# A graph network on one core: where the turn of a gathered block's sums and the MLP's steps stand among the dense steps

## The chip, the cores and the metric

One NeuronCore of a Trainium2 chip. The metric is the device time of one execution in microseconds (us), lower is better. The engines are named as in the profile: PE (TensorE, matmuls; PEld is its weight load), DVE (VectorE), ACT (ScalarE), POOL (GpSimd) and SP (SyncE, whose queue issues most DMAs). Each engine runs its own instructions in the order in which the program issued them.

## The reference

6250 nodes with 256 channels, 100,000 edges with random ends, sorted by destination, four layers of neighbour sums and a three-step MLP:

```
h = relu(layernorm(x))
for l in range(3):
    g = h + segment_sum(h[src], dst)
    g = relu(g @ W1s[l] + b1s[l])
    g = relu(g @ W2s[l] + b2s[l])
    h = g @ W3s[l] + b3s[l]
g = h + segment_sum(h[src], dst)
g = relu(g @ cW1 + cb1); g = relu(g @ cW2 + cb2)      # 256 -> 64 channels
out = x + g @ cW3 + cb3
```

## The kernel before

**Two ways to sum neighbours.** The nodes are cut into 49 blocks of 128 (`NT` = 49). A layer's sums are made in two ways at once. Most blocks are *dense*: the adjacency matrix of a panel of three or four blocks is built once as 8-bit counts and kept in DRAM (`mats`), and every layer multiplies it with all node rows. The others (`gone`: blocks 0 to 18 and 48, in layer 0 also 44 to 47) are *gathered*: their edges' source rows are fetched by indirect DMAs on POOL (`send`, L1183, tile `rows`), and one-hot matrices (`hot`, DVE, L1210) add them up on PE (`add`, L1236, tile `sums` in PSUM). In this kernel the first linear step W1 is already multiplied into the rows, so the sums need only a bias and relu to become the MLP's `h1`.

**The dense step is the clock of the program.** `product` runs a panel in 49 steps, one for each source block j. A step issues four matmuls L1330 (two halves of the channels, times a high and a low part of the rows, which are kept in SBUF as `XY`) against one tile `a` of the matrix. `a` is cast from 8 bits by `prepare`, three steps ahead: in layer 0 always on ACT (L1306), later on ACT for even j and on DVE for odd j (L1308). Its ring has seven buffers from layer 1 on (five in layer 0). There are 7 panels in layer 0 and 8 in each of layers 1 to 3: 31 x 49 = 1519 steps, 6076 matmuls.

**Everything else is hung on steps.** `tick` counts a step and issues what is due; `later(n, f)` makes f due n steps from now. At each step the order is: what is due, then the gathering (`advance`), then the casts (`prepare`), then the four matmuls. A gathered block has two visits (`add`), each 24 or 20 small matmuls. After the second comes `finish`:

- one step later DVE adds `sums` to `u` (L1248), and `after` makes this add wait for the last matmul of the step that follows the sums (`paced`);
- three steps later (two for block 48, the last) `turn` transposes `u` into `pt` on PE (L1259); every second block, or at a group's end, ACT makes `h1` of it (L1263);
- after the last block of a group of up to four, `mlp` is called.

`u` itself starts as the sum of the block's own rows, high and low part, which DVE makes at the *first* visit (L1223). Where these rows are no longer needed, `used` says so and `reload` may bring in the next layer's rows: a DMA on SP's queue into `back`, and five steps later `split` on ACT (L1037) and DVE (L1038), three blocks at a time.

**The MLP** serves gathered groups and dense panels alike. `start` is the step of its first products (`second`, L1081, into `ps`); ACT makes `h2` two steps later (L1083); the last products (`third`, L1104, in the last layer L1101) follow, then DVE adds the bias (L1113, L1109) and SP stores (L502, L507). `free` keeps two MLPs apart. `hurry` marks the two at a layer's end, the last panel's and block 48's. When all 49 blocks of a layer are stored, `begin` starts the next layer's gathering, spread evenly over the steps that are left.

Of the kernel before, what the change touches and what calls it, by code (L numbers as in the profile page):

```python
# [8 lines left out]
F32 = mybir.dt.float32  # L9
# [5 lines left out]
OP = mybir.AluOpType  # L15
PSUM = bass.MemoryType.PSUM
DRAM = bass.MemoryType.DRAM
P = 128
# [378 lines left out]
def sorted_edges(  # L397
# [38 lines left out]
    nc = tc.nc  # L436
    N, C = x.shape
# [28 lines left out]
    gone = [(0, 4), (4, 4), (8, 4), (12, 4), (16, 3), (44, 4), (48, 1)]  # L466
# [14 lines left out]
    XY = const.tile([P, NT, 2 * C], F32R, name="XY")  # L481
# [400 lines left out]
    with tc.manual_schedule():  # L882
        with tc.tile_pool(name="prep", bufs=2) as prep, tc.tile_pool(
            name="ps_t", bufs=2, space=PSUM
# [29 lines left out]
        work = ctx.enter_context(tc.tile_pool(name="work", bufs=1))  # L914
# [104 lines left out]
        due, now, free = [], [0], [0]  # L1019

        def later(n, fn):
            due.append((now[0] + n, fn))
# [9 lines left out]
        used, kept, wanted, lent = set(), set(), [], [0]  # L1032
# [8 lines left out]
        def reload(l, j):  # L1041

            if (l, j) in used and (l, j) in kept and l < NLAYER:
                wanted.append((l, j))
                bring()
# [20 lines left out]
        def mlp(l, b0, n, h1, hurry):  # L1066

            w = n * P
            end = l == NLAYER
            mid = NOUT if end else C  # L1070
            mp = min(mid, P)
            start = max(now[0] + 2 - hurry, free[0])
            free[0] = start + (5 + (n + 1) // 2 if hurry else 8)
            h2 = []

            def second(i):
                if i == 0:
                    h2.append(work.tile([P, KC, W], F32, name="h2"))
                ps = ps_m.tile([P, W], F32, name="ps")
                for c in range(KC):  # L1080
                    nc.tensor.matmul(ps[:mp, :w], weights[l][0][:, c, i * P:i * P + mp],  # L1081
                                     h1[:, c, :w], start=(c == 0), stop=(c == KC - 1))
                later(2, lambda: nc.scalar.activation(h2[0][:mp, i, :w], ps[:mp, :w], AF.Relu,  # L1083
                                                      bias=b2[l][:mp, i:i + 1]))

            def third(i):
                m = min(2, n - i)
                w3 = weights[l][1]
                if end:
                    xt = late.tile([P, 2, C], F32, name="xt", bufs=3)  # L1090
                    if b0 + i + m == NT and LAST < P:
                        nc.vector.memset(xt[:, m - 1, :], 0.0)
                    rows_io(x, b0 + i, m, xt, True)
                    nc.vector.tensor_tensor(xt[:, :m, :], xt[:, :m, :],
                                            w3[1][:, None, :].to_broadcast([P, m, C]), OP.add)
                ps = ps_m.tile([P, W], F32, name="ps")
                for q in range(m):
                    nodes = slice((i + q) * P, (i + q + 1) * P)
                    o = ps[:, q * C:(q + 1) * C]
                    if end:  # L1100
                        nc.tensor.matmul(o, h2[0][:mp, 0, nodes], w3[0], start=True, stop=True)  # L1101
                    else:
                        for c in range(KC):
                            nc.tensor.matmul(o, h2[0][:, c, nodes], w3[:, c, :],  # L1104
                                             start=(c == 0), stop=(c == KC - 1))
                v = ps[:, :m * C].rearrange("p (q c) -> p q c", c=C)
                if end:
                    z = late.tile([P, 2, C], F32, name="z", bufs=2)
                    later(2, lambda: nc.vector.tensor_tensor(z[:, :m, :], v, xt[:, :m, :], OP.add))  # L1109
                    later(4, lambda: rows_io(out, b0 + i, m, z, False))  # L1110
                    return
                z = work.tile([P, 2, C], F32, name="zz", bufs=3)
                later(2, lambda: nc.vector.tensor_tensor(  # L1113
                    z[:, :m, :], v, w3[:, KC:, :].to_broadcast([P, m, C]), OP.add))

                def store():
                    rows_io(tables[l + 1], b0 + i, m, z, False)
                    blocks = range(b0 + i, b0 + i + m)
                    kept.update((l, j) for j in blocks)
                    if all((l, j) in used for j in blocks):  # L1120
                        split(b0 + i, m, z)
                    else:
                        for j in blocks:
                            reload(l, j)
                    if sum(1 for k, _ in kept if k == l) == NT:
                        layers[l + 1].begin(now[0])
                        later(1, lambda: load_weights(l + 1))

                later(3 - hurry, store)

            def at(t, fn):
                due.append((t, fn))

            for i in range(-(-mid // P)):
                at(start + i, lambda i=i: second(i))
            for i in range(0, n, 2):
                at(start + 5 - hurry + i // 2, lambda i=i: third(i))


        def after(ins, reason):  # L1140
# [9 lines left out]
        class Gathered:  # L1150
# [65 lines left out]
            def add(self):  # L1216
                v = self.done
                g, rounds = self.visits[v]
                b, n, i, _ = self.blocks[g]
                if rounds[0] == 0:  # L1220
                    self.sums = sums
                    self.u = work.tile([P, C], F32, name="u", bufs=1)
                    nc.vector.tensor_tensor(self.u, XY[:, b + i, :C].bitcast(F32),  # L1223
                                            XY[:, b + i, C:].bitcast(F32), OP.add)
                    used.add((self.l, b + i, 0))
                    if (self.l, b + i, 1) in used:
                        used.add((self.l, b + i))
                        reload(self.l, b + i)
                if v == 0:
                    self.one_hots(0)  # L1230
                end = rounds[-1] == len(ROUNDS) - 1
                for r in rounds:
                    for h in range(2):
                        for m, k in enumerate(ROUNDS[r]):
                            if k is not None:
                                nc.tensor.matmul(  # L1236
                                    self.sums[(2 * h + m) * Q:(2 * h + m + 1) * Q, :C],
                                    self.hots[r, m][:, h, :], self.rows[g, h, k], start=(r == 0),
                                    stop=(r == (len(ROUNDS) - 2 if m == 0 else len(ROUNDS) - 1)))
                self.done += 1  # L1240
                if self.done < self.n:
                    self.one_hots(self.done)
                if end:
                    self.finish(b, n, i, self.sums)

            def finish(self, b, n, g, sums):
                u = self.u
                later(1, lambda: after(nc.vector.tensor_tensor(u, u, sums[:, :C], OP.add),  # L1248
                                       "a full product stands behind the sums"))
                if g == 0:  # L1250
                    self.h1 = work.tile([P, KC, W], F32, name="h1", bufs=2)
                h1 = self.h1

                def turn():
                    if g % 2 == 0:
                        self.pt = ps_g.tile([P, KC, 2 * P], F32, name="pt")
                    i = g % 2
                    for c in range(KC):
                        nc.tensor.transpose(self.pt[:, c, i * P:(i + 1) * P],  # L1259
                                            u[:, c * P:(c + 1) * P], ident)  # L1260
                    if i == 1 or g == n - 1:
                        for c in range(KC):
                            nc.scalar.activation(h1[:, c, (g - i) * P:(g + 1) * P],  # L1263
                                                 self.pt[:, c, :(i + 1) * P], AF.Relu,
                                                 bias=b1[self.l][:, c:c + 1])
                    if g == n - 1:
                        mlp(self.l, b, n, h1, b == gone[-1][0])

                later(2 if b == gone[-1][0] else 3, turn)

# [5 lines left out]
        paced = []  # L1278
        sums = ps_g.tile([P, W], F32, name="sums")
        LEAD, TAIL = 75, 8  # L1280

        ends = [PRE + NT * sum(k + 1 for k in last[:l + 1]) for l in range(NLAYER + 1)]
        when = [0.0]
# [79 lines left out]
        with tc.tile_pool(name="hots", bufs=1) as hots, tc.tile_pool(  # L1363
            name="ats", bufs=1
        ) as ats, tc.tile_pool(name="rings", bufs=AHEAD + 2) as rings, tc.tile_pool(
            name="gath", bufs=24
# [90 lines left out]
```

## Time and profile before

| | |
|---|---|
| runs shown, us | 2673.98, 2686.91, 2672.84 (median 2673.98) |
| the profiled execution, us | 2672.19 |
| its span, first to last instruction, us | 2670.4 |
| mean granted TensorE clock | 0.934 |
| ACT casts L1306, DVE casts L1308 | 943 of 579 ns, 576 of 480 ns |
| DVE adds of own rows L1223, of sums L1248 | 84 of 419 ns, 84 of 420 ns |
| dense products L1330: four and three tiles wide | 3724 and 2352 |
| POOL row gathers L1183 | 1512 of 985 ns |

A line of the costliest groups gives line, engine, operation, tiles written and read, shapes and count; then busy us in all and mean ns of one; then the engine's idle time just before these instructions, and what ended it. In a timeline a line is a run of like instructions of one engine: start, length in us, engine, line, and in brackets the idle time before it and its releaser. The span falls into preparation (until about 270 us), layer 0 (until about 930 us) and three layers of about 580 us each. Matmul ends are modelled, so the time at which a matmul's signal reaches another engine has to be read from that engine.

### The profile page before, as it was taken

To read this page: it belongs to the slowest core of one execution; us is meant where nothing else is said; L and a number is where in the kernel's file an instruction comes from. 1 tells how busy PE (TensorE), PEld (TensorE's weight loads), DVE (VectorE), ACT (ScalarE), POOL (GpSimd) and SP (SyncE) were. 2 spreads that over 40 slices of the span, in tenths; PEclk is the share of its full clock that TensorE was granted. 3 is DMA by queue.
4 is the path that set the end of the run, shared out by engine and by line. 5 is a ranking of instruction groups with operands and counts; after the bars stand their busy time and mean duration, and the time that the engine had idled before them with its cause. 6 is when DMAs were issued, how large, how long until landed. Compare 5 with 4: busy or idle time off the path is not lost.

```text
span 2670.4 us, 35208 instructions
## 1 busy us (share of the span) xinstructions
PE 2252.3 (84%) x12356; PEld 1610.3 (60%) x12356; DVE 934.6 (35%) x2806; ACT 915.6 (34%) x1917; POOL 1541.8 (58%) x1586
## 2 busy tenths in 40 slices
PE   4374888998888988999899988898889899898897
PEld 2252665655665665666666666666766765566655
DVE  6245553533554432222223422222323422233222
ACT  3352654544555532222222422222223322222221
POOL 3305666656656366666666366665666366666663
PEclk8685998999998999999999999998999999999899
DMA  4223544544545554544445554444445555455543
GB/s 137 64 77 123 175 153 142 183 132 137 164 148 169 160 175 132 157 134 134 143 129 171 157 153 122 132 145 121 146 146 157 166 149 158 142 153 159 153 138 106
DMA packets 252048, 383.44 MB, mean 144 GB/s; under 512 B 35190, under 2 KB 198200, under 8 KB 251860
## 3 DMA queue, kind: packets, MB, share of 16 engines
q0 software_dynamic: 74176, 200.88, 25.8%
q1 hardware_dynamic: 175758, 178.36, 21.4%
q8 instruction: 99, 1.62, 0.3%
q10 hardware_dynamic: 1926, 1.85, 0.2%
q14 instruction: 89, 0.73, 0.1%
HBM read 324.49 MB, written 56.46 MB: 143 GB/s over the span
## 4 chain that ended last, share of the span: by engine, by line
PE 70%; another core or an unknown queue 11%; issue 9%; ACT 3%; DVE 3%; DMA 3%; POOL 1%; SPq 0%; ACTq 0%; DVEq 0%; POOLq 0%
PE agg L1330 44%; PE sums L1236 8%; PE ps L1081 6%; PE ps L1104 5%; PE bp L992 4%; DMA rows<-table,idx 2%; PE pt L1259 1%; POOL rows L1183 1%; PE ps L1101 1%; ACT at L999 1%; ACT a L1306 1%; PE bp L847 1%; DVE u L1248 0%; DVE hot L1210 0%
## 5 line engine op out<-in xcount | busy, mean ns | idle before, releaser
L1183 POOL DMA_INDIRECT rows<-table,idx x1512 | 1489.9, 985 | 1001.0 <-PE agg L1330 353.8
L1330 PE MATMUL agg<-a,XY 128*128 128x512 f32 (+1 forms) x6076 | 1517.9, 396 | 44.7 <-issue 26.3
L1330 PEld LDWEIGHTS agg<-a,XY 128*128 128x128 f32 x6076 | 1119.3, 196 | 306.9 <-issue 132.7
L1306 ACT CAST a<-at 128x512 fp32r<-128x512 uint8 (+1 forms) x943 | 531.9, 579 | 822.9 <-PE agg L1330 564.6
L1308 DVE CAST a<-at 128x512 fp32r<-128x512 uint8 (+1 forms) x576 | 266.0, 480 | 523.4 <-PE agg L1330 386.1
L1236 PE MATMUL sums<-rows,hot 128*32 128x256 f32 x3696 | 300.6, 393 | 44.0 <-DMA rows<-table,idx 28.3
L999 ACT CAST at<-bp 128x392 uint8<-128x392 f32 x348 | 162.5, 490 | 239.0 <-PE bp L992 121.3
L1236 PEld LDWEIGHTS sums<-rows,hot 128*32 128x32 f32 x3696 | 122.7, 111 | 196.4 <-issue 92.5
L1248 DVE TENSOR_TENSOR u<-u,sums 128x256 f32<-128x256 f32 x84 | 35.3, 420 | 568.1 <-PE agg L1330 310.1
L992 PE MATMUL bp<-hi,lo 128*128 128x196 bf16 x928 | 146.4, 266 | 88.9 <-ACT at L999 50.7
L1081 PE MATMUL ps<-h,w 128*128 128x512 f32 (+5 forms) x392 | 183.8, 595 | 27.7 <-ACT h L1263 13.2
L992 PEld LDWEIGHTS <-lo 128*128 128x128 bf16 x928 | 77.3, 102 | 176.7 <-issue 132.0
L1210 DVE TENSOR_TENSOR hot<-colf,rel 128x64 f32<-128x64 f32 x924 | 139.2, 216 | 15.3 <-PE agg L1330 6.6
L1104 PE MATMUL ps<-w,h 128*128 128x256 f32 x588 | 140.3, 379 | 0.8 <-issue 0.8
L951 DVE TENSOR_TENSOR lo<-lanes,pairs 128x512 bf16<-128x512 bf16 x232 | 97.2, 419 | 109.6 <-issue 42.3
L1263 ACT ACTIVATE h<-pt,bias 128x256 f32<-128x256 f32 (+1 forms) x92 | 36.9, 453 | 286.5 <-PE pt L1259 200.2
L951 DVE TENSOR_TENSOR hi<-cols,pairs 128x784 bf16<-128x784 bf16 x232 | 129.5, 558 | 0.0
L1081 PEld LDWEIGHTS ps<-h,w 128*128 128x128 f32 (+1 forms) x392 | 74.1, 199 | 89.3 <-issue 41.5
L1259 PE MATMUL pt<-ident,u 128*128 128x128 f32 x168 | 38.3, 313 | 104.0 <-DVE u L1248 67.1
L1104 PEld LDWEIGHTS ps<-w,h 128*128 128x128 f32 x588 | 111.0, 189 | 17.1 <-issue 1.2
L1001 DVE CAST at<-bp 128x392 uint8<-128x392 f32 x116 | 65.5, 565 | 140.0 <-PE bp L992 72.0
L1083 ACT ACTIVATE h<-ps,bias 128x512 f32<-128x512 f32 (+5 forms) x98 | 62.4, 637 | 122.2 <-PE ps L1081 95.2
(136 smaller groups left out, 796.8 us busy)
## 6 DMA issues: line engine op xcount, KB each, us to landing
at<-mat SPq DMA_DIRECT2D x133, 448.0 KB
at<-mat SPq DMA_DIRECT2D x84, 336.0 KB
rows<-table,idx POOLq DMA_INDIRECT x1512
mat<-at SPq DMA_DIRECT2D x29, 784.0 KB
table<-zz SPq DMA_DIRECT2D x66, 256.0 KB
back<-table SPq DMA_DIRECT2D x126, 128.0 KB
xs<-in_x_dram SPq DMA_DIRECT2D x8, 768.0 KB
table<-zs SPq DMA_DIRECT2D x24, 256.0 KB
```

Source lines behind the costliest of these rows:

```text
L951: nc.vector.tensor_tensor(o.rearrange("p q (n t) -> p q n t", t=2), values.rearrange("p (n t) -> p n t", t=2)[:, None, :, :].to_broadcast( ...
L992: nc.tensor.matmul(bp[:, m * HW:(m + 1) * HW], lo[:, q + m, :], hi[:, q + m, :], start=True, stop=True)
L999: nc.scalar.copy(o, v)
L1001: nc.vector.tensor_copy(o, v)
L1081: nc.tensor.matmul(ps[:mp, :w], weights[l][0][:, c, i * P:i * P + mp], h1[:, c, :w], start=(c == 0), stop=(c == KC - 1))
L1104: nc.tensor.matmul(o, h2[0][:, c, nodes], w3[:, c, :], start=(c == 0), stop=(c == KC - 1))
L1183: got = nc.gpsimd.indirect_dma_start(out=t, out_offset=None, in_=tables[self.l][:, :], in_offset=bass.IndirectOffsetOnAxis(ap=idx[:, o:o + ...
L1210: nc.vector.tensor_tensor(hot[:, i, :, :], colf[:, None, i * Q:(i + 1) * Q].to_broadcast([P, 2, Q]), rel[:, o + k:o + k + TS + 1:TS, None] ...
L1236: nc.tensor.matmul(self.sums[(2 * h + m) * Q:(2 * h + m + 1) * Q, :C], self.hots[r, m][:, h, :], self.rows[g, h, k], start=(r == 0), stop= ...
L1306: nc.scalar.copy(o, mat[l, p][j])
L1308: nc.vector.tensor_copy(o, mat[l, p][j])
L1330: mm = nc.tensor.matmul(agg[c][:, :w], XY[:, j, o:o + P], a[:, :w], start=(j == 0 and half == 0), stop=(j == NT - 1 and half == 1))
```

## The change

It moves four things and leaves every instruction's form and their number as they are. With `FAR` = 7:

- `turn` stands 7 steps behind `finish` and no longer 3; block 48's stays at 2.
- An MLP without `hurry` starts 5 steps after it is called (before 2), and its last products follow 9 steps after the start (before 5). With `hurry` these distances stay 1 and 4.
- `free` becomes start + apart + half the blocks, rounded up, + 2 (1 with hurry): 13 steps for a group or panel of three or four blocks (before 8); with hurry as before.
- The sum of own rows into `u`, with the `used` and `reload` that belong to it, is issued in `finish`, after the second visit, and no longer at the first.

```diff
--- before.py
+++ after.py
@@ -1069,8 +1069,9 @@
             end = l == NLAYER
             mid = NOUT if end else C
             mp = min(mid, P)
-            start = max(now[0] + 2 - hurry, free[0])
-            free[0] = start + (5 + (n + 1) // 2 if hurry else 8)
+            start = max(now[0] + (1 if hurry else FAR - 2), free[0])
+            apart = 4 if hurry else FAR + 2
+            free[0] = start + apart + (n + 1) // 2 + (1 if hurry else 2)
             h2 = []
 
             def second(i):
@@ -1134,7 +1135,7 @@
             for i in range(-(-mid // P)):
                 at(start + i, lambda i=i: second(i))
             for i in range(0, n, 2):
-                at(start + 5 - hurry + i // 2, lambda i=i: third(i))
+                at(start + apart + i // 2, lambda i=i: third(i))
 
 
         def after(ins, reason):
@@ -1219,13 +1220,6 @@
                 b, n, i, _ = self.blocks[g]
                 if rounds[0] == 0:
                     self.sums = sums
-                    self.u = work.tile([P, C], F32, name="u", bufs=1)
-                    nc.vector.tensor_tensor(self.u, XY[:, b + i, :C].bitcast(F32),
-                                            XY[:, b + i, C:].bitcast(F32), OP.add)
-                    used.add((self.l, b + i, 0))
-                    if (self.l, b + i, 1) in used:
-                        used.add((self.l, b + i))
-                        reload(self.l, b + i)
                 if v == 0:
                     self.one_hots(0)
                 end = rounds[-1] == len(ROUNDS) - 1
@@ -1244,7 +1238,13 @@
                     self.finish(b, n, i, self.sums)
 
             def finish(self, b, n, g, sums):
-                u = self.u
+                u = work.tile([P, C], F32, name="u", bufs=1)
+                nc.vector.tensor_tensor(u, XY[:, b + g, :C].bitcast(F32),
+                                        XY[:, b + g, C:].bitcast(F32), OP.add)
+                used.add((self.l, b + g, 0))
+                if (self.l, b + g, 1) in used:
+                    used.add((self.l, b + g))
+                    reload(self.l, b + g)
                 later(1, lambda: after(nc.vector.tensor_tensor(u, u, sums[:, :C], OP.add),
                                        "a full product stands behind the sums"))
                 if g == 0:
@@ -1266,7 +1266,7 @@
                     if g == n - 1:
                         mlp(self.l, b, n, h1, b == gone[-1][0])
 
-                later(2 if b == gone[-1][0] else 3, turn)
+                later(2 if b == gone[-1][0] else FAR, turn)
 
 
 
@@ -1278,6 +1278,7 @@
         paced = []
         sums = ps_g.tile([P, W], F32, name="sums")
         LEAD, TAIL = 75, 8
+        FAR = 7
 
         ends = [PRE + NT * sum(k + 1 for k in last[:l + 1]) for l in range(NLAYER + 1)]
         when = [0.0]
```

## The prediction

> **What bounds the kernel now.** I read the page's busy times and its chain first, then what TensorE (PE) waited for, then the order of time around one gathered block, then the clock by windows, and last the end of the run.
>
> The page:
> ```profile
> span 2670.4 us, 35208 instructions
> PE 2252.3 (84%) x12356; PEld 1610.3 (60%) x12356; DVE 934.6 (35%) x2806; ACT 915.6 (34%) x1917; POOL 1541.8 (58%) x1586
> ...
> PE 70%; another core or an unknown queue 11%; issue 9%; ACT 3%; DVE 3%; DMA 3%; POOL 1%; SPq 0%; ACTq 0%; DVEq 0%; POOLq 0%
> ...
> L1259 PE MATMUL pt<-ident,u 128*128 128x128 f32 x168 | 38.3, 313 | 104.0 <-DVE u L1248 67.1 <-issue 36.7
> ```
> PE is the bound: 84% busy and 70% of the chain. It is idle for 418 us, and the largest single part, 104.0 us, lies before the transposes L1259 of a gathered block's sums. The waits of PE, dearest in total first (total, times, longest):
> ```profile
> PE pt L1259 <- DVE u L1248: 67.1, 29, 4.4
> ...
> PE pt L1259 <- issue: 36.7, 19, 3.8
> ...
> PE ps L1081 <- ACT h L1263: 13.2, 3, 4.9
> ...
> PE ps L1081 <- ACT h L1346: 10.8, 11, 3.4
> ```
> The first two are the turn, the last two the MLP's first step behind what it reads. These are the two waits that the change moves away from. One block, in order of time:
> ```profile
> 1711.58 1.50 PE L1236 MATMUL sums<-rows,hot 128*32 128x256 f32 x20
> ...
> 1713.01 3.08 PE L1330 MATMUL agg<-a,XY 128*128 128x512 f32 x12
> ...
> 1719.88 0.42 DVE L1248 TENSOR_TENSOR u<-u,sums 128x256 f32<-128x256 f32 x1 [10.64 <-remote]
> ...
> 1720.22 1.10 DVE L1308 CAST a<-at 128x512 fp32r<-128x512 uint8 x3
> ...
> 1720.36 0.44 PE L1259 MATMUL pt<-ident,u 128*128 128x128 f32 x2 [4.27 <-DVE u L1248]
> ```
> After the sums PE runs three dense steps (12 products), then stands for 4.27 us until VectorE (DVE) has added u. The add waits for the first of the three steps (a dependency written by hand in `after`), which ended near 1714.0. It starts at 1719.88, so the step's signal is some 5.7 us late. Over all blocks that have products before them I take the add's start less the modelled end of that step: median 2.7 us, longest 6.7. Why the signal is late the trace doesn't tell. The clock around it (columns: us, busy us and instructions of PE, PEld, DVE, ACT, POOL, granted clock, DMA share, GB/s):
> ```profile
> 1715.00:1720.00 5.00, 1.09 (x5) 0.56 (x3) 0.12 (x1) 0.01 (x1) 2.45 (x3) 1.00 0.35 104
> 1720.00:1725.00 5.00, 4.64 (x15) 3.69 (x16) 2.75 (x11) 0.90 (x2) 3.95 (x4) 0.66 0.28 76
> ```
> The wait costs twice: behind it the granted clock falls to 0.66 over 5 us. In the trace's clock records it is at half in 54 stretches, 354 us in all.
>
> A visit without a turn shows what PE does when nothing of its own waits for that signal:
> ```profile
> 1420.36 1.50 PE L1236 MATMUL sums<-rows,hot 128*32 128x256 f32 x24
> ...
> 1421.80 4.95 PE L1330 MATMUL agg<-a,XY 128*128 128x512 f32 x20
> ...
> 1426.64 1.10 DVE L1308 CAST a<-at 128x512 fp32r<-128x512 uint8 x3 [6.48 <-PE agg L1330]
> ...
> 1427.54 1.98 PE L1081 MATMUL ps<-h,w 128*128 128x512 f32 x4 [0.80 <-ACT h L1346]
> ```
> DVE is released equally late (1426.64), yet PE went on for five steps and stood 0.80 us.
>
> **The change, part by part.** No instruction is added or taken away: 84 adds of own rows (L1223, 419 ns), 84 adds of sums (L1248, 420 ns), 168 transposes, and the MLP's products stay. They move.
>
> *Turn at +7 (before +3).* PE no longer stands at the third step. But the add keeps its wait and its place on DVE, and DVE works in order. From layer 1 on, odd steps' casts L1308 are DVE's. The first cast behind the add is for the fifth product after the sums or the sixth, by parity, so PE needs it after four steps or five. For each of the 57 blocks of layers 1 to 3 (block 48 aside, whose turn stays at +2) I leave the add where the trace has it and ask when the cast is ready: add 0.42 + cast 0.43 + 0.10 for two signals. Against that stands PE's arrival: its third step's end as in the trace, and one or two steps more of 0.935 us (four tiles wide) or 0.70 (three). In the block above: ready 1719.88 + 0.95 = 1720.83; PE there at 1716.1 + 0.94 = 1717.0; it stands 3.8 us in place of 4.27. Over the 57 blocks 44 waits of 96.3 us become 37 of 61.2 us: **-35 us**. Bounds: 0 if PE meets the same wait wherever it stands, -91 if the casts ahead suffice as in the visit without a turn. I take the middle, since the queue's order is certain and the release time is the trace's own. In layer 0 all casts are ACT's (ScalarE's), and five turn waits sum to 7.7 us; behind the add stand the one-hot builds that PE's L992 needs soon: **-4** (bounds 0 and -7.7).
>
> The Trainium skill ("TensorE: Matmul & The Clock Gate", Architectural detail) says that ACT and DVE queues are strictly first in, first out; this speaks against the change, and the trace agrees: three casts start 0.34 us after the add and none before it. By that rule the turn can stand as late as it likes, and the add's own wait still reaches PE.
>
> *Clock behind these waits.* 18 half-clock stretches in layers 1 to 3 follow a turn's wait, 85 us, of which PE loses half, about 42. Waits over 2 us fall from 21 to 16, and I take a third of the stretches off: **-14** (bounds 0 and -42). The same page's Part 1 gives a window of about 3.4 us of idleness before the clock halves. The stretches here are whole multiples of 3.41 us, but a wait of 1.88 us at 1111 is followed by one as well; by the page's rule only the longest waits would cost clock, and the term would be some 10 us smaller.
>
> *MLP steps.* The first step stands 5 steps behind the turn or the panel's end (before 2), the third stage 9 behind the first (before 5). Three more steps are 2.1 to 2.8 us. The three L1263 waits (13.2) fall to about 4.7, the eleven L1346 waits (mean 1.0) to about 0.6: **-18** (bounds 0, -24). Four half-clock stretches (20.5 us) follow such waits: **-7** (0, -10).
>
> *Own rows at the end.* The add L1223 moves from the first visit to behind the second, ahead of the paced add. DVE idles before L1248 for 568 us in all, which hides 0.42 us each; without that cover it would be 84 x 0.42 = 35 us on DVE. Reloads of XY for blocks 16 to 18 come up to 12 steps later: by the step numbers of the code their XY is there 18 steps before the next layer reads it (before 29 or more), and the tightest tiles (39 in layer 0, 42 in the others) keep 5 and 8 steps. The reload DMAs on SP's queue are issued in the same number or a few fewer: 0.
>
> *Layer ends.* MLPs now hold each other off by 13 steps (before 8). Worked through the code's counters, block 48's MLP starts 9 (layer 0) or 5 steps later than it asks, the last panel's too, so the next layer's gather begins 9 or 5 steps later and must be 1 to 2% denser; POOL is 58% busy: 0. Bounds: 0 to +6 a layer, nine steps of 0.7 us, were the gather late.
>
> *The end of the run.* Block 48's third stage falls behind the last product. Before, its output left SP at 2658.30 and the last loads of x followed it at 2659.08, the head of the closing chain. Now that output waits for the h2 step on ACT behind the panel's h (0.69 + 0.36), its own load of x (2.16 to landing) and two adds: loads some 3.0 us later, less 0.6 us of PE work that leaves the path: **+2.5** (bounds 0, +4).
>
> Sum: -35 -4 -14 -18 -7 +2.5 = -75.5. The profiled execution took 2672.2 us (span 2670.4 and 1.8 around it), the median shown is 2674.0, 1.8 above. 2674 - 75 = **2599 us**, own range 2560 to 2640.
>
> **Rivals.**
> *The casts ahead suffice.* Blocks behave as the visit at 1420: PE runs through the late signal. For it: over layers 1 to 3 the nine steps after a visit without a turn lose 0.75 us together, after one with a turn 3.9. Against it: there no add sits ahead of the casts. -91 -7 -42 -28 +2.5 = -165: 2508.
> *The wait goes to the ring.* Signals come later still once PE never stops to let them catch up; a cast for step s reuses the buffer of step s-7, and PE stands there instead. For it: signals are late after most sums, and on time (0.01 us) where an MLP's long products ran just before. Against: in the visit at 1420 it cost little. Only the MLP's terms are left, half of them: about 2660, own range 2640 to 2687.
> *Slower: the release follows the stop.* If the late signal comes only a fixed time after PE has run dry, PE stops for the missing cast instead of for u, as long as now, and then needs add and cast (0.95) in place of add alone (0.47). 49 stops x 0.48 = +24, +2.5 at the end, and the MLP's waits stay: 2700. It decides from the point where most releases come after PE's stop. For it: in the block above all three steps' signals arrive together, late in the stop. Against: around 1537 DVE and ACT were released while PE ran 12 steps without a break.
> *The change doesn't reach its aim at layer ends* (hurried MLPs held back): priced above at 6 us a layer at most, inside every case.
>
> **How the numbers follow.** First case 0.47, casts suffice 0.15, ring 0.22, slower 0.16. Half a per cent (2661 to 2687) is about what a measurement here can tell from no change. Faster: 0.47 + 0.15 + half of the ring's, 0.11 = 0.73; same: 0.09 of the ring's and 0.02 of the last = 0.11; slower 0.16. The range 2520 to 2692 leaves out most of the second case and most of the slower one's upper part.
>
> **What would show it.** Right: idle before L1259 near nothing, a new wait of PE's L1330 on DVE's L1308 of some 60 us, half-clock time down by a fifth or more, L1081 waits below 8 us, the last loads of x near 3 us later against the last product. Wrong: L1330 gains no wait (second case), or gains 90 us or more (third, fourth), or POOL's rows arrive late at the layers' first sums.

## The result, and the profile after

The changed kernel takes 2642.2 us (median of four, 2634.39 to 2647.98), the kernel before 2673.4 (four, 2666.89 to 2686.91): ratio 0.9883, 95% interval 0.9853 to 0.9912, or 31 us less. The forecast was 2599, 75 us less. Every ratio below is against runs of the kernel before on the same chip beside it. The chips showed two conditions, a first in which the kernel before takes 2666 to 2703 us (medians) and a second in which it takes 2298 to 2306; before and after and the first eight experiments are of the first, and where one is of the second, this is said.

The page after:
```profile
span 2635.5 us, 35153 instructions
PE 2257.3 (86%) x12356; PEld 1616.9 (61%) x12356; DVE 933.8 (35%) x2804; ACT 907.4 (34%) x1915; POOL 1547.9 (59%) x1586
...
L1331 PE MATMUL agg<-a,XY 128*128 128x512 f32 (+1 forms) x6076 | 1527.9, 397 | 127.1 <-issue 55.1
...
L1230 PE MATMUL sums<-rows,hot 128*32 128x256 f32 x3696 | 312.4, 393 | 50.7 <-issue 26.4
...
L1082 PE MATMUL ps<-h,w 128*128 128x512 f32 (+5 forms) x392 | 169.6, 555 | 4.0 <-DVE z L1110 2.3
```
PE is as busy as before (2257 us against 2252). What it stood for has moved: before the dense products (L1331, L1330 of the kernel before) it is idle for 127.1 us, where it was 44.7; before the MLP's first step 4.0, where it was 27.7; before the sums 50.7, where it was 44.0. The chain of waits can't be set beside that of before, since it was followed back over only a fifth of the span.

PE's waits after (total, times, longest), in order of size, those of the preparation and of the building of the panels in layer 0 left out:
```profile
PE agg L1331 <- issue: 55.1, 94, 3.3
PE agg L1331 <- DVE a L1309: 35.8, 22, 4.3
...
PE sums L1230 <- issue: 26.4, 41, 1.9
...
PE sums L1230 <- DMA rows<-table,idx: 22.4, 23, 2.1
PE agg L1331 <- ACT h L1347: 18.2, 5, 7.3
...
PE agg L1331 <- DVE u L1248: 11.3, 6, 2.9
```
The turn L1259, 104 us before, is not in the list; in the view of that line alone it stands with 2.2 us. In its place PE waits for DVE's casts, for ACT's reading of the panel's products, and for "issue", time with no releaser that the profile shows (55.1 us before the dense products, where it was 26.3).

One block, in order of time (start, length, engine, line; in brackets the idle time before it and its releaser):
```profile
2338.57 1.07 PE L1230 MATMUL sums<-rows,hot 128*32 128x256 f32 x16
2339.67 0.95 POOL L1184 DMA_INDIRECT rows<-table,idx  x1 [0.30 <-issue]
...
2340.81 3.29 PE L1331 MATMUL agg<-a,XY 128*128 128x512 f32 x16
...
2343.43 0.95 POOL L1184 DMA_INDIRECT rows<-table,idx  x1 [0.30 <-issue]
2346.43 1.26 ACT L1347 ACTIVATE h<-agg,bias 128x512 f32<-128x512 f32 x2 [9.99 <-remote]
2346.47 0.42 DVE L1248 TENSOR_TENSOR u<-u,sums 128x256 f32<-128x256 f32 x1 [9.84 <-remote]
2346.70 0.95 POOL L1184 DMA_INDIRECT rows<-table,idx  x1 [2.31 <-remote]
2346.81 1.92 DVE L1309 CAST a<-at 128x384 fp32r<-128x384 uint8 x4
2347.41 1.65 PE L1331 MATMUL agg<-a,XY 128*128 128x384 f32 x4 [3.31 <-DVE a L1309]
```
The turn is away, and the stop is here all the same. PE ends its products near 2344.1; ACT, DVE and POOL, which wait for PE's signals, are all released at 2346.4 to 2346.7 ("remote": a signal came, and the profile finds no instruction that ended shortly before it); DVE adds, then casts four tiles in a row, and PE has stood 3.31 us for the first of them. POOL had issued gathers without a pause until 2344.4.

Layers 1 to 3 added up from the matmul records: for each kind of product the time PE spends on it, and behind the stroke the idle time before it (us). The two middle columns are the first two experiments.

| | before | turn alone | MLP alone | both (after) |
|---|---|---|---|---|
| dense products | 1117 / 22 | 1114 / 63 | 1109 / 28 | 1119 / 93 |
| sums | 211 / 40 | 231 / 58 | 212 / 44 | 222 / 48 |
| turn | 12 / 96 | 12 / 0 | 12 / 90 | 13 / 0 |
| MLP's first step | 103 / 25 | 106 / 29 | 98 / 3 | 98 / 4 |
| time of layers 1 to 3 | 1729 | 1718 | 1702 | 1703 |

The MLP's last products, 106 to 111 us in every column, are left out. The turn alone was profiled in an execution of 2661 us, the shortest of its twelve, so its 1718 is no sign of a gain. In layer 0, which takes 658, 664, 660 and 652 us in this order, the change takes away the turn's 7.7 us, and the idle time before the dense products rises from 22 to 34. Seven of the 35 us between the two profiled executions lie in the preparation, which the change doesn't touch.

### The profile page after: what moved, and what is told of

Read it like the earlier page. It is cut to its first block, busy times and chain, and to the rows that moved or that the text cites. A ratio compares the mean times of both kernels' runs of the same rounds, so it can differ in the third digit from the quotient of the medians.

```text
span 2635.5 us, 35153 instructions
## 1 busy us (share of the span) xinstructions
PE 2257.3 (86%) x12356; PEld 1616.9 (61%) x12356; DVE 933.8 (35%) x2804; ACT 907.4 (34%) x1915; POOL 1547.9 (59%) x1586
## 5 line engine op out<-in xcount | busy, mean ns | idle before, releaser
L1331 PE MATMUL agg<-a,XY 128*128 128x512 f32 (+1 forms) x6076 | 1527.9, 397 | 127.1 <-issue 55.1
L1331 PEld LDWEIGHTS agg<-a,XY 128*128 128x128 f32 x6076 | 1122.0, 196 | 408.3 <-issue 166.1
L1307 ACT CAST a<-at 128x512 fp32r<-128x512 uint8 (+1 forms) x943 | 525.3, 579 | 936.7 <-PE agg L1331 560.6
L1230 PE MATMUL sums<-rows,hot 128*32 128x256 f32 x3696 | 312.4, 393 | 50.7 <-issue 26.4
L1082 PE MATMUL ps<-h,w 128*128 128x512 f32 (+5 forms) x392 | 169.6, 555 | 4.0 <-DVE z L1110 2.3
L1114 DVE TENSOR_TENSOR zz<-ps,w 128x512 f32<-128x512 f32 (+1 forms) x81 | 51.5, 638 | 95.7 <-PE ps L1105 67.3
```

The costliest lines, as they stand in the source:

```text
L1230: nc.tensor.matmul(self.sums[(2 * h + m) * Q:(2 * h + m + 1) * Q, :C], self.hots[r, m][:, h, :], self.rows[g, h, k], start=(r == 0), stop= ...
L1307: nc.scalar.copy(o, mat[l, p][j])
L1331: mm = nc.tensor.matmul(agg[c][:, :w], XY[:, j, o:o + P], a[:, :w], start=(j == 0 and half == 0), stop=(j == NT - 1 and half == 1))
```

## The experiments

**Which half of the change does it.** The turn's new place and the own rows alone (the MLP's distances put back), and the MLP's distances alone in the kernel before:
```diff
 turn alone, against the changed kernel (the third stage's step goes back likewise)
-            start = max(now[0] + (1 if hurry else FAR - 2), free[0])
-            apart = 4 if hurry else FAR + 2
-            free[0] = start + apart + (n + 1) // 2 + (1 if hurry else 2)
+            start = max(now[0] + 2 - hurry, free[0])
+            free[0] = start + (5 + (n + 1) // 2 if hurry else 8)
 MLP alone, against the kernel before: the same lines the other way
```


> The turn at +7 and the own rows in finish, as in the changed kernel; the MLP's steps as before. Theory A (the turn's wait moves to the casts behind the add on DVE, the MLP's steps are a gain of their own): PE's idle before L1259 is near 0, its idle before the dense products near 120 us as in the changed kernel, its idle before the MLP's first products near 25 us as before; ratio to before 0.994 (some -15 us). Theory B (the MLP's steps do nothing without the turn, all gain is the turn's): ratio 0.988 as the changed kernel.

> The MLP's steps alone; the turn at +3 and the own rows at the first visit, as before. Theory A: PE's idle before L1259 stays near 104 us, its idle before the MLP's first products falls from 27.7 to below 8 us, ratio 0.992 (some -20 us). Theory B: ratio 1.000.


Measured: turn alone 1.0022 (0.9995 to 1.0049), no gain; MLP alone 0.9874 (0.9834 to 0.9915), all of it. Two of the waits with the turn alone:
```profile
PE agg L1330 <- issue: 49.1, 69, 4.1
...
PE ps L1081 <- ACT h L1346: 28.1, 17, 5.6
```
The turn's 96 us in layers 1 to 3 are gone, and 41 of them stand before the dense products, 18 before the sums, 4 before the MLP; the sums' own time grows by some 20 us. So theory A was right that the MLP's steps are a gain of their own, though it gave them 0.992, and that the wait goes to the dense products, though these have 90.6 us over the whole run where it had 120; it was too kind to the turn (it gave 0.994). Theory B fell.

**Is it DVE's order?** The add issued five steps behind the sums, so that two casts stand ahead of it (`after` gets the step to wait for as an argument); and the casts prepared five steps ahead from layer 1 on, with two buffers more for them and four fewer, 22, for gathered rows:
```diff
-                later(1, lambda: after(nc.vector.tensor_tensor(u, u, sums[:, :C], OP.add),
-                                       "a full product stands behind the sums"))
+                behind = []
+                later(1, lambda: behind.extend(paced))
+                later(1 if b == gone[-1][0] else 5, lambda: after(
+                    nc.vector.tensor_tensor(u, u, sums[:, :C], OP.add),
+                    "a full product stands behind the sums", behind))
 the other one
-                prepare(u + 1 + AHEAD)
+                prepare(u + 1 + (AHEAD if late is None else AHEAD + 2))
```


> The changed kernel, with DVE's add of the sums issued five steps behind finish and no longer one, waiting for the same dense step as there; so the casts of the steps between stand ahead of it on DVE. Theory A (the order on DVE makes the new wait): PE's idle before the dense products in layers 1 to 3 falls from 92 us to below 45, ratio to before below 0.978. Theory R (the late signals stop PE through the ring of casts, whatever the order): that idle stays above 75 us and the ratio stays within 0.984 to 0.992.

> The changed kernel with casts five steps ahead from layer 1 on (before three), a ring of nine buffers (seven) and 22 buffers for gathered rows (26). The first cast behind the add is then needed seven or eight steps after the sums. Theory A: PE's idle before the dense products in layers 1 to 3 falls below 45 us, ratio to before below 0.978. Theory S (the release of the late signals follows PE's stop): that idle stays above 75 us, ratio 0.984 or more. If gathered rows come late for want of buffers, PE's idle before the sums grows beyond 60 us.


Measured: 0.9897 (0.9863 to 0.993) and 0.9888 (0.9849 to 0.9927), like the change itself. The idle time before the dense products in layers 1 to 3 did fall, from 93 to 57 and 57 us, but the sums took 237 and 242 us in place of 222, and stood 66 and 72 us in place of 48 (in the second run the fewer buffers for rows may have a share in that). The order on DVE says where PE stops, and hardly how long it stops in all.

**Do the rows come too late?** Each gather asked for 30 of the planner's units earlier, in four kernels (`LEAD + 30` in `advance`): the changed one, the one before, the late add, and the MLP alone.


> The changed kernel with gathered rows asked for some five steps earlier (30 more in the lead of 75). Theory P (what the turn's wait gave up is taken back by gathered rows that come too late for their sums): PE's time on and before the sums in layers 1 to 3 falls from 270 us to below 235, ratio to before below 0.978. Theory Q (PE meets the late signals anyway, the sums only share the same time): the sums' time may fall, but the waits before the dense products rise by as much, ratio 0.984 to 0.992 as the changed kernel.

> The kernel before with the same earlier rows. Theory P: the turn's waits give the rows time already, so little is gained: the sums' time in layers 1 to 3 falls from 251 us to about 230, ratio 0.990 to 0.997. Theory Q: no change, 1.000.

> The changed kernel with DVE's add five steps behind finish (as e3_add_late) and with the earlier rows. Theory P: in e3 the sums' time was 303 us in layers 1 to 3; here below 240, with the waits before the dense products near 57 us as there: the best of all, ratio below 0.970. Theory Q: ratio 0.984 to 0.992.

> The MLP's steps alone (as e2_mlp_only) with the earlier rows, turn at +3. Theory P: ratio some 0.005 below e2's 0.987, about 0.982, above those of the two with the turn moved and rows early. Theory Q: 0.987.


Measured: 0.998 (0.9958 to 1.0003), 1.009 (1.0067 to 1.0114), 0.9978 (0.9953 to 1.0002), 0.9984 (0.996 to 1.0007): all four lose about one per cent against themselves. Between the start of a visit's last gather and its sums lie some 12 us in place of 3 to 4, and in the changed kernel the sums' wait falls from 48 to 19 us; yet the dense products' rises from 93 to 142. P fell; Q had the waits right and missed the loss. Half clock grows with it (424 us in place of 331 in the changed kernel, 431 in place of 354 in the one before); why was not followed up.

**Is PE still at work when its records have ended?** If so the late signals were hidden work. Spare products behind the end of the changed kernel answer it:
```diff
+        def quads(n, only=None):
+            for k in range(n):
+                m = k % 4 if only is None else only
+                nc.tensor.matmul(sums[m * Q:(m + 1) * Q, :C], hs[k % len(hs)][:, k // 4 % 2, :],
+                                 rs[k % len(rs)], start=True, stop=True)
...
+        quads(480)
+        mark(sums)
+        quads(120, 0)
+        mark(sums)
+        dense(240)
```


> The changed kernel with spare matmuls behind its end, whose results go nowhere: 100 dense products, then 480 of the sums' small matmuls in fours (as in a visit), 120 of them on one and the same quarter, 240 dense products, and twenty times 24 small ones followed by 12 dense; between the parts VectorE copies what was written and TensorE waits for that copy. Question: do VectorE's signals come late behind the sums because TensorE is really still busy with them, longer than its records show? Theory M (hidden work): the records give a visit's small matmuls 54 ns apiece (four start together, the next four 217 ns later), but TensorE needs twice to four times that, 110 to 215 ns; the 480 then last 52 to 103 us by VectorE's copy, and a mixed round of 24 + 12 takes 1.3 to 3.9 us longer than by its records so that the twenty rounds last 105 to 160 us. Theory L (a late signal, no work): the 480 last 26 us, the 120 on one quarter 26 us, a mixed round 4 us or less, twenty of them about 80 us, and the copies follow the last record within 3 us, or up to 7 late behind the mixed part.


Measured: 480 in fours last 52.9 us from copy to copy, 120 on one quarter 52.8, the twenty mixed rounds 115.6. That looks like the low end of theory M, but each of the small products stands in the trace as two records (960 and 240), and for the 480 that is 55 ns a record, as in the layers (220 on one quarter). I had counted records as products, also in the description of the kernel: the 24 or 20 of a visit are 12 or 10 products. The copies follow the last modelled end by less than 0.1 us: no hidden work on this chip, theory L. The surprise was beside it: here the kernel before took 2306 us, and PE was idle for 1.0 us before L1333, the dense products.

**The same kernels in the other condition.**


> The kernel before, unchanged, profiled once more beside the changed one. The run with the spare matmuls had come with a kernel before of 2306 us where all other comparisons had some 2665, and in its trace VectorE was released 0.01 us behind the sums, not 2.5 us. Theory C (the late signals are a condition of the chip, not of the kernel's order): where the kernel before takes some 2306 us, its waits before L1259 fall from 104 us to under 10 and no stretch of half clock stands behind a turn; where it takes some 2665, they are 90 us or more again. Theory K (the order of the work makes them): 60 us or more on either chip.

> The changed kernel, unchanged. Theory C: on a chip of 2306 us there is little for the change to remove, ratio to before 0.990 to 1.000, idle of PE before L1331 below 10 us; on one of 2665 us 0.985 to 0.992 as at first, idle above 100. Theory K: 0.985 to 0.992 on either.

> The kernel before with the MLP's steps moved alone. Theory C: on a chip of 2306 us 0.995 to 1.002, since no late signal is there to step back from; on one of 2665 us 0.984 to 0.992. Theory K: 0.984 to 0.992 on either.


These three ran in the second condition (before 2301.2 us). Against that the kernel before comes out at 0.9998 (0.9977 to 1.0018), the change at 1.0009 (0.9991 to 1.0026), the MLP's part alone at 0.998 (0.9961 to 0.9998). The page of the kernel before, there:
```profile
span 2304.7 us, 35208 instructions
PE 2151.3 (93%) x12356; PEld 1574.8 (68%) x12356; DVE 945.5 (41%) x2806; ACT 921.5 (40%) x1917; POOL 1547.8 (67%) x1586
...
L1330 PE MATMUL agg<-a,XY 128*128 128x512 f32 (+1 forms) x6076 | 1465.6, 389 | 0.7 <-ACT a L1306 0.3
...
L1236 PE MATMUL sums<-rows,hot 128*32 128x256 f32 x3696 | 299.2, 388 | 62.0 <-DMA rows<-table,idx 59.7
```
The same instructions, and no wait before L1259 at all. The first signal behind the sums comes 0.01 us after its product's modelled end (1.4 us after first visits and 2.6 after second ones in the first condition). Half clock holds for 125 us against 354. So theory C: there is nothing for this change to remove, and the turn's half, if anything, costs a little: 1.0009 with it, 0.998 without.

**What makes the signals late?** Spare rounds of 12 dense products, each round's result read by ACT, behind 0, 12 and 24 small products; first in the second condition, then in the first (before 2670.5 us):


> The changed kernel with spare matmuls behind its end, results unused: 100 dense products; 480 of the sums' small matmuls in fours; 120 on one quarter; then three times twenty rounds of 12 dense products each, behind 0, 12 (as a visit has) and 24 small matmuls, where ScalarE copies a strip of every round's result, so that the start of this copy shows when the round's signal came; no transfer of the layers runs beside it. Theory T (where signals are late, the traffic of the layers makes them so): copies start within 0.5 us of their round's modelled end in all three parts, on either chip. Theory G (on a chip of 2665 us, small matmuls ahead of dense products are enough): the parts with 12 and 24 small ones show copies 1.5 us late or more, the part without below 0.5; on a chip of 2306 us none.

> The same kernel as the second one with spare matmuls, once more, in the hope of a chip on which the kernel before takes some 2665 us. There: Theory T (the layers' traffic makes the signals late): ScalarE's copies start within 0.5 us of their round's modelled end in all three parts, as on the chip of 2301 us. Theory G (small matmuls ahead of dense products are enough): with 12 and 24 small ones the copies are 1.5 us late or more, without them below 0.5. Theory R (TensorE itself is slower than its records show, whatever it runs): the 480 small ones, the dense rounds and the mixed rounds all last longer by VectorE's copies than on the chip of 2301 us (52.0, 57 and 89 us there), by a tenth or more.


From copy to copy the parts last 52.87, 52.82, 57.39, 89.95 and 115.83 us in the one, and 52.87, 52.82, 57.39, 89.96 and 115.83 in the other; no copy is more than 0.37 us late in either. With nothing beside it PE is not slower, and sums ahead of dense products do nothing by themselves. That leaves what the layers run beside PE:
```diff
...
+        rounds(20, 0)
+        gathers(40, mark(ds[1]))
+        rounds(20, 0)
+        mark(ds[1])
+        rounds(20, 0, 1)
+        loads(12, mark(ds[1]))
+        rounds(20, 0)
+        gathers(60, mark(ds[1]))
+        rounds(20, 12)
+        mark(ds[1])
+        rounds(20, 0)
```


> The changed kernel with six parts of spare work behind its end, results unused. Each has twenty rounds of 12 dense products, ScalarE copying a strip of every round's result, some 57 us: (1) alone; (2) beside 40 row gathers that GpSimd issues back to back; (3) with one gather a round, each waiting for its round's last product; (4) beside 12 loads of 448 KB on SP's queue; (5) with 12 of the sums' small matmuls ahead of each round's products (90 us) and 60 gathers back to back; (6) alone again. In the traces of the layers on a chip where the kernel before takes 2665 us, TensorE's signal behind the sums is 2.6 to 3.2 us late on average where GpSimd is in the middle of a chain of gathers, and 0.3 to 0.6 us where it pauses. Theory P (GpSimd's gathers hold TensorE's signals up): on such a chip the copies of parts 2 and 5 start 2 us late or more, up to the length of the chain (51 and 77 us), until GpSimd stops; part 3 at most 1.5 us late; parts 1, 4 and 6 within 0.4 us. Theory D (transfers of any kind do): part 4 is late too. Theory N (neither): all within 0.4 us. On a chip of 2301 us all parts are within 0.4 us under each theory.

> The same six parts once more, for a chip on which the kernel before takes some 2665 us. Theory P (GpSimd's back-to-back gathers hold TensorE's signals up): parts 2 and 5 show copies 2 us late or more, up to the end of the chain; part 3 (one gather a round) at most 1.5 us; parts 1, 4 and 6 within 0.4. Theory D (transfers of any kind): part 4 is late too. Theory N (neither): all within 0.4 us.


The first of the two was of the second kind (before 2300.2): every copy within 0.37 us, parts 1, 2, 3, 4 and 6 56.5 us long from the first dense product to the last copy, part 5 87.5. Part 2 there in order of time, ACT's copies beside the gathers:
```profile
2374.95 0.95 POOL L1434 DMA_INDIRECT rows<-table,idx  x1 [0.30 <-issue]
2375.02 0.17 ACT L1451 COPY z<-agg 128x16 f32<-128x16 f32 x1 [3.75 <-PE agg L1449]
...
2377.88 0.17 ACT L1451 COPY z<-agg 128x16 f32<-128x16 f32 x1 [2.69 <-PE agg L1449]
...
2380.69 0.17 ACT L1451 COPY z<-agg 128x16 f32<-128x16 f32 x1 [2.64 <-PE agg L1449]
```
A copy every 2.8 us, as PE ends its rounds. The second was of the first kind (before 2703.0). The same part there:
```profile
2745.14 17.02 PE L1449 MATMUL agg<-a,XY 128*128 128x512 f32 x72
2745.58 0.95 POOL L1434 DMA_INDIRECT rows<-table,idx  x1 [102.24 <-PE agg L1411]
...
2757.69 0.17 ACT L1451 COPY z<-agg 128x16 f32<-128x16 f32 x1 [3.69 <-PE agg L1449]
...
2768.28 0.17 ACT L1451 COPY z<-agg 128x16 f32<-128x16 f32 x1 [10.42 <-remote]
2768.50 4.77 PEld L1449 LDWEIGHTS agg<-a,XY 128*128 128x128 f32 x12 [6.78 <-issue]
2768.50 5.48 PE L1449 MATMUL agg<-a,XY 128*128 128x512 f32 x12 [6.34 <-issue]
...
2794.61 0.95 POOL L1434 DMA_INDIRECT rows<-table,idx  x1 [0.30 <-issue]
2796.33 0.17 ACT L1451 COPY z<-agg 128x16 f32<-128x16 f32 x1 [27.88 <-remote]
2796.55 3.48 PEld L1449 LDWEIGHTS agg<-a,XY 128*128 128x128 f32 x9 [23.28 <-issue]
2796.55 3.78 PE L1449 MATMUL agg<-a,XY 128*128 128x512 f32 x8 [22.57 <-issue]
...
2802.00 0.30 ACT L1451 COPY z<-agg 128x16 f32<-128x16 f32 x2 [5.50 <-PE agg L1449]
```
Three rounds come on time; then the copies are 1.1, 8.9, 34.2 and 28.0 us late. The one at 2796.33 comes 0.8 us after the end of the fortieth gather, the last; the next, whose product ended at 2773.98, comes 6.4 us after it, together with the copy of the round behind it, and from there on they are on time. PE itself goes on until both of its result tiles wait for ACT, then stands 6.3 and 22.6 us. ACT's signal to PE is not held up: at 2768.50, amid the gathers, PE goes on 0.05 us after the copy's end. Part 2 lasts 91.2 us in place of 56.5; part 5, with 60 gathers, has copies 20.5 and 43.0 us late and lasts 159.6 in place of 87.5. One gather a round, the loads on SP's queue, and the empty parts: nothing over 0.37 us. Theory P.

The traces show one thing more, which none of the theories had. In part 5 PE slows down itself, beside the gathers, before instructions that by their records wait for no semaphore:
```profile
2957.93 3.08 PE L1449 MATMUL agg<-a,XY 128*128 128x512 f32 x12
...
2982.88 0.58 PE L1449 MATMUL agg<-a,XY 128*128 128x512 f32 x1 [2.21 <-issue]
2985.71 0.58 PE L1449 MATMUL agg<-a,XY 128*128 128x512 f32 x1 [2.24 <-issue]
2987.81 0.58 PE L1449 MATMUL agg<-a,XY 128*128 128x512 f32 x1 [1.52 <-issue]
```
The third round's twelve products take 23 us in place of 3.1, though their result tile has been free since 2956.9; most of them start at steps of 0.70 us or a multiple of it. The layers have such stops as well: in layers 1 to 3 PE stands before instructions that wait for no semaphore 34 times and 14 us in the kernel before, 52 and 26 with the turn alone, 38 and 18 with the MLP alone, 80 and 40 in the changed kernel, 105 and 52 with the late add. In the second condition (the same three kernels: before, changed, MLP alone) there is not one. What makes them is not shown.

**The same in the layers.** Every second gather left out in the kernel before, twice; the second half of a tile's edges is then summed with the first half's rows:
```diff
+                    if h:
+                        self.rows[g, h, k] = self.rows[g, 0, k]
+                        self.sent += 1
+                        continue
```


> The kernel before with every second row gather left out: the second half of a tile's edges is summed with the first half's rows, so half of the gathered neighbours' sums are missing from the result; every matmul, cast and step stays. GpSimd then issues one gather where it issued two and pauses between them. Theory P (GpSimd's chains of gathers hold TensorE's signals up, and that is where the turn's waits come from): on a chip where the kernel before takes 2665 us it falls to 2280 to 2420, the idle time before L1259 from some 100 us to under 20, and the signal behind the sums is late by less than 0.6 us on average; on a chip of 2301 us it falls by no more than 70, the waits for rows. Theory M (the chains matter, but most of the loss is elsewhere): 2450 to 2600 on the first kind. Theory N (they do not matter in the layers): 2600 or more, idle before L1259 of 60 us or more.

> The same kernel once more, with every second row gather left out, for a chip on which the kernel before takes some 2665 us. On the chip of 2304 us it fell by 114 us, 44 more than the most I had allowed, to 2189. Theory P (GpSimd's chains hold the signals up in the layers too): 2190 to 2300 here as well, that is 370 to 480 below the kernel before; idle before L1259 under 20 us; the signal behind the sums late by less than 0.6 us. Theory M: 2350 to 2500. Theory N: it falls by 114 us as there, to about 2550, and the idle time before L1259 stays at 60 us or more.


Both times the chip was of the second kind: 2189.4 us against 2303.6 (0.9512, 0.9472 to 0.9551) and 2188.8 against 2298.5 (0.9521, 0.9505 to 0.9537). Half of the gathers cost 4.9% and 4.8% there, more than I had allowed (waits for rows, 37 us in layers 1 to 3, are gone, and the sums run 31 us faster); what leaving them out does in the first condition, where the question lies, was not seen and stays open.

## Why the prediction was right in sign and wrong in size

**The step that failed** is "Turn at +7", -35 us, with its clock term -14 and layer 0's -4, -53 in all. The turn alone measured 1.0022: about +6, between -1 and +13. That the wait would leave its place was right, idle before L1259 went from 104 us to 2. What failed is the sentence "I leave the add where the trace has it". The time of the release is not the trace's own: with the turn alone, signals behind first visits come 2.5 us late, where they were 1.4 (2.8 in the full change). Before, the stop at the turn was where PE sat out the lateness, and the next visit started clean. Without the stop PE runs on and meets the held-up signals a little later, at a cast, at a panel's end or at the sums; that it is the same lateness which PE meets there is argued from these numbers. So not "a new wait of PE's L1330 on DVE's L1308 of some 60 us", but in the changed kernel 36 on the casts, 35 on ACT and the add, and 55 with no releaser shown (26 before). Part of this stands before products that wait for no signal at all: over all of PE's products in layers 1 to 3 such stops grew from 14 to 26 us by the turn alone, a loss that the prediction had no term for.

**The MLP's steps**, -18 and -7: the MLP's part alone gave 0.9874, -34 us (-44 to -23). Right, if a little small. L1081's waits fell to 4.0 us (forecast: below 8). An MLP's products wait for signals as well, and 3 to 4 more steps, 2 to 4 us, outlast most lateness of 1 to 3 us; here little of the stop moved elsewhere, the dense products' idle time rose by 6 us only.

**The clock** was to lose a fifth of its half-clock time; it went from 354 to 331 us, 6%. The stops moved, and the clock falls behind them where they are now: 0.68 in the 4 us from 2348, behind the stop shown above.

**The end of the run**, +2.5: from the start of the last dense product to the issue of the last store 12.4 us where it was 8.2, and the last loads of x follow it 5.6 us later in place of 2.3. The step is right, a little small (+4.2), and only both halves together make it: each alone ends in 8.2 to 8.3. The move of the own rows and the layers' ends were not tried by themselves.

**The rivals.** "The wait goes to the ring" comes nearest to what happened: signals later still once PE never stops, and only the MLP's terms left. How much of the wait stands at the ring's buffers, as it had it, was not measured. It gave 2660 with 2640 to 2687, since it counted half of these terms. I weighed it 0.22 against 0.47 because the visit at 1420 cost little; one visit is not the mean. "The casts ahead suffice" fell with the casts five steps ahead; "the release follows the stop" fell with the turn alone, which lost nothing like 24 us.

**Where the lateness comes from.** In the prediction I wrote that the trace doesn't tell. It had a hint. In the block shown there POOL's last gather ends at 1718.06 and the add starts at 1719.88. Over layers 1 to 3 of the kernel before, the signal behind the sums is 2.6 us late on average where POOL is in a run of gathers when it is due (88 visits), 0.3 where it isn't (32); after the change 2.9 (104) and 0.5 (16). This alone proves little, since POOL's gathers wait for PE's signals too and pause when these are late. The spare work has no such loop, and there back-to-back gathers held the signals up, and nothing else that was tried did. The preparation, which has no sums, shows it as well: two of ACT's copies in the kernel before wait there for products that ended before 73 us, beside a run of indirect transfers up to 101.1; the first is released amid the run, the second 2.2 us after it.
```profile
92.18 0.36 ACT L734 CAST clT<-ps 128x240 bf16<-128x240 f32 x1 [20.60 <-issue]
...
100.23 0.91 POOL L702 DMA_INDIRECT near_i<-in_src_dram,from_i  x1 [0.30 <-issue]
103.38 0.36 ACT L734 CAST clT<-ps 128x240 bf16<-128x240 f32 x1 [10.84 <-remote]
```
That the layers' late signals have this one cause is likely from these, and not shown by a run in the layers. What sets the condition of the chip is open.

A version as good as the change, and simpler, is the MLP's part alone: 0.9874 against 0.9883 in the first condition, 0.998 against 1.0009 in the second.

## What to carry to other kernels

A wait at one instruction can be the place where an engine sits out a delay that comes from elsewhere; before moving the instruction, ask what the signal itself was waiting for, and who else stands behind the same signal. A release time read from the trace of before may be kept in a sum only when its cause is known. When signals are late, look at what runs on the engines that take no part in the wait, and time the pieces by themselves, with and without that work beside them. Time that a profile gives to no releaser deserves a look of its own: here part of it stands before instructions that had nothing to wait for.

## What the runs showed of the hardware

- In one condition of the chip, back-to-back indirect gathers of GpSimd (0.95 us each, 0.30 apart) held TensorE's completion signals up for as long as 34 us (40 gathers) and 43 us (60); beside the 40 the first three rounds, 8 us, were still on time, and the last held-up copy came 6.4 us after the last gather (9.5 beside the 60). One gather in 2.8 us, and 12 loads of 448 KB on SP's queue, held nothing up. In the other condition none of them did.
- Beside the 60 gathers TensorE's own instructions, with no semaphore to wait for, came mostly at steps of 0.70 us or a multiple: twelve products took 23 us in place of 3.1. The layers have 34 such stops in the kernel before and 80 in the changed one in that condition, none in the other.
- With no gathers beside it TensorE's rates are the same in both: five spare parts of 53 to 116 us agree to 0.01 us. The kernel before takes 2301 us in one and 2670 in the other with 12,356 matmul records in each.
- The Trainium skill ("Perfetto Trace Analysis", Tensor Engine Instruction) says that the profile's end of a matmul is an estimate, and that the signal goes out after PSUM's acknowledgement and then has to propagate. The trace agrees that there are such steps behind the end: 0.01 to 0.37 us in one condition, up to 43 us in the other.
